# When the projections of a transposed block are queued in a four-layer graph network, and four edits of its first group

## The chip, the cores and the metric

The kernel runs on one core of a Trainium2 chip. Its time is device microseconds of one execution of the whole program; the reported number is the median of three runs. The profile is of one further execution.

## The reference

Four graph layers are applied to node features `x` (3327 x 256, float32) with one dense 0/1 adjacency `adj` (3327 x 3327). Each is wrapped as `x = layernorm(x + layer(x, adj))`. Cut to what matters:

```python
# layer 0: cosine attention, half of it kept
Qn, Kn = norm(x @ Wq.T), norm(x @ Wk.T)
att = softmax(where(adj > 0, Kn @ Qn.T, NEG), axis=1)
out0 = 0.5 * (att @ x) + 0.5 * x            # rows without neighbours keep x
# layer 1 and each of the three passes of layer 3 (3a, 3b, 3c): additive attention
h  = x @ W
e  = leaky_relu(h @ a[:D] + (h @ a[D:]).T, 0.01)
out = elu(softmax(where(adj > 0, e, NEG), axis=1) @ h)
# layer 2: dot-product attention
q, k, v = x @ Wq.T + bq, x @ Wk.T + bk, x @ Wv.T + bv
out2 = elu(softmax(where(adj > 0, q @ k.T / 16, NEG), axis=1) @ v)
```

Layer 3 first multiplies by `W0`, then makes the three passes, each on the result of the one before; only the end of the third is added to `x` and normalised.

## The kernel before, in words

**Tiles and loops.** The nodes are padded to 3328 = 26 tiles of 128 (`NT`). Rows are worked on in `NB` = 7 blocks: b = 0 to 5 have 512 rows (four tiles), b = 6 has 256 (two tiles). The program is one list of steps (layer, b, j): for each of six layer passes (keys "0", "1", "2", "3a", "3b", "3c"), each block b and each key tile j = 0 to 25. A step adds `e.T @ V[j]` to the accumulators `po` of the block, one matmul for each row tile (L1331; L1316 in the very last block of 3c; seven half-size products in L779 for layer 2 and the middle blocks of layer 0). A float32 matmul appears as two rows in the record. There are five `po` banks and three other banks (`bank()`, tag `pb`) of the accumulator memory.

**Weights ahead of their use.** The attention weights `e` of a step are made two steps earlier: ScalarE makes `re` (L657), VectorE multiplies it by the adjacency mask (L668). Before that a pass needs `th`, `rh`, `nrh` for its keys and `u` for the block's rows. They come from the end of the pass before: `shift` (a maximum on VectorE L606, a maximum over partitions on GpSimd L608, five small VectorE operations), `keys` (L623 to L627) and `block` (L649).

**Finishing a block.** `finish` is a generator that works on block b while the next block's steps run. `advance()` is called once at the end of each step and moves it to its next `yield`. For layers 1 and 3 it scales the accumulators into `p4` (L957, which frees the `po` banks), and then `turn` transposes `p4` by DMA. That is: ScalarE copies the two 16-bit halves into `planes` (L834), SP's queue issues the transposing DMA (L837), the generator yields `steps` times, and VectorE copies the arrived planes into `pT` (L844). After that each row tile is projected by TensorE with the layer's weights (`projected`, L988) and activated. So the number `steps` decides after which step's matmuls the first projection stands in the program. It is 3 for b = 0 to 4; for b = 5 and b = 6 it is 5 in layer 1 and 6 in layer 3. Block 5 is finished during block 6, whose steps hold half the matmuls; block 6 is finished during the first block of the next pass. At the end of block 5 come `shift`, `keys` and `rows` for the next pass.

In layer 1 the normalised block is turned a second time (L1063), for the keys of layer 2; that call has its own step numbers.

At step j = 20 (25 in the last block of layer 1) whatever is still pending is drained at once.

**Who sets the order.** Up to the fourth step the order of TensorE, ScalarE, VectorE and GpSimd is written by hand (`manual_schedule`). After that a planner orders each engine's instructions: it keeps its own model of how long things take, and of the instructions that this model says are ready it takes the one that comes first in the program. Each engine then runs its list in order, with semaphores. DMAs are issued from SP's queue, the first one also from ScalarE's.

**The start.** Six matmuls of ones (`turned`, "fills", L80) run first, then four that make the identity. `queries0(0)` multiplies the features into `pk` (two banks), takes lengths on ScalarE (L368) and an inverse root on VectorE (`rk`), scales the four tiles (`kr`: tile 0 on ScalarE L390, tiles 1 to 3 on VectorE L388), and transposes them on TensorE (`pkT`, L394). `keys0(0)` makes `pq` (L317), squares it on ScalarE (`qsq`, L324), copies it (L325), sums the squares with eight small matmul rows into `pn` (L329), and VectorE makes the inverse root `rq`, after the first adjacency mask (`take_adj`). The order of the two generators is a list in the main program:

```python
    for part in (k0, q0, k0, q0, q0, k0, k0, q0, q1):
        next(part, None)
```

## Time and profile before

| | |
|---|---|
| median of three runs | 2369.26 us (2368.96 to 2370.93) |
| profiled execution, its time | 2369.43 us |
| its span, first to last instruction | 2367.6 us |
| granted TensorE clock, mean | 0.998 |
| TensorE matmul, busy | 2343.5 us (99%) |
| TensorE weight loads, busy | 1914.2 us (81%) |
| VectorE, busy | 1598.5 us (68%) |
| ScalarE, busy | 1222.4 us (52%) |
| GpSimd, busy | 39.9 us (2%) |
| DMA, mean rate | 91 GB/s |

PE stands for TensorE, PEld for its weight loads, ACT for ScalarE, DVE for VectorE, POOL for GpSimd, SP for the engine whose queue issues DMAs. A row of a timeline reads: start in us, length in us, engine, line, operation, what is written from what is read, shape, number of instructions, and in brackets the idle time before it with what ended it. A row of waits reads: who waited for whom, us in total, times, longest. Matmuls are pipelined and the record models their ends, so TensorE's 99% says that it is always occupied and not that it is at its peak.

### The profile page before, as it was taken

The numbers are of one execution on the slowest core, as the hardware profiler recorded it, in microseconds if no ns is written. First come the engines' busy times: TensorE is split into PE (matmuls) and PEld (weight loads), VectorE is DVE, ScalarE is ACT, GpSimd is POOL, SyncE is SP. The second block draws the span as 40 slices with busy tenths as digits, with TensorE's granted clock in tenths as the row PEclk, the third lists the DMA queues.
The fourth block names the chain that finished last, engine by engine and source line by source line (L and its number), as shares of the span: only waits on it lengthen the run. The fifth ranks groups of instructions, "written<-read, shape, count | busy, mean of one in ns | idle before, by whom it ended". The sixth has DMA issues, their size and how long they took to land.

```text
span 2367.6 us, 33122 instructions
## 1 busy us (share of the span) xinstructions
PE 2343.5 (99%) x11961; PEld 1914.2 (81%) x11961; DVE 1598.5 (68%) x4246; ACT 1222.4 (52%) x1958; POOL 39.9 (2%) x156
## 2 busy tenths in 40 slices
PE   9999999999999999999999999999999999999997
PEld 6788888888888777667667798888888888888886
DVE  7789999856666667566566685556556555655655
ACT  4677777755555422222222255555655555655554
POOL 0000001000000000000000000000000000000000
PEclk9999999999999999999999999999999999999999
DMA  8655555413332312212212222211211111122120
GB/s 274 192 191 186 168 191 194 158 62 83 83 78 57 107 50 87 83 50 88 77 46 73 84 83 52 72 52 26 79 44 43 45 57 52 49 93 69 61 66 23
DMA packets 147288, 214.66 MB, mean 91 GB/s; under 512 B 76093, under 2 KB 101172, under 8 KB 142516
## 3 DMA queue, kind: packets, MB, share of 16 engines
q1 hardware_dynamic: 146852, 212.28, 29.2%
q8 instruction: 94, 1.54, 0.3%
q14 instruction: 70, 0.57, 0.1%
q10 hardware_dynamic: 272, 0.26, 0.0%
HBM read 167.53 MB, written 28.19 MB: 83 GB/s over the span
## 4 chain that ended last, share of the span: by engine, by line
PE 96%; DVE 2%; DMA 1%; ACT 1%; issue 0%; SPq 0%; POOL 0%; DVEq 0%; ACTq 0%
PE po L1331 50%; PE po L779 20%; PE ps L563 12%; PE ps L492 6%; PE pproj L988 4%; PE pv L1074 1%; PE pgq L522 1%; PE po L1316 1%; PE pk L353 1%; DMA stage<-in_adj_a 0%; PE pq L317 0%; DVE v L668 0%; DVE e L506 0%; DVE acc L449 0%; PE pn L329 0%
## 5 line engine op out<-in xcount | busy, mean ns | idle before, releaser
L1331 PE MATMUL po<-v,e 128*128 128x257 f32 x5616 | 1251.8, 381 | 1.5 <-ACT p L957 1.4
L1331 PEld LDWEIGHTS po<-v,e 128*128 128x128 f32 x5616 | 1062.1, 190 | 168.6 <-ACT p L957 9.4
L657 ACT ACTIVATE re<-u,nrh,th 128x512 f32<-128x512 f32 (+1 forms) x728 | 555.0, 780 | 479.2 <-DVE e L668 474.7
L668 DVE SCALAR_TENSOR_TENSOR e<-re,rh,mask 128x512 f32<-128x512 f32 (+1 forms) x702 | 501.1, 719 | 375.8 <-PE po L1331 353.1
L563 PE MATMUL ps<-gT,ft 128*128 128x512 f32 (+1 forms) x728 | 307.4, 563 | 0.0
L571 ACT ACTIVATE ex<-ps,off 128x512 f32<-128x512 f32 (+1 forms) x182 | 119.1, 656 | 357.2 <-PE ps L563 356.5
L779 PE MATMUL po<-tsums,ssum 128*128 128x128 f32 (+1 forms) x1794 | 249.3, 275 | 0.0
L477 DVE SCALAR_TENSOR_TENSOR e<-ex,mask 128x512 f32<-128x512 f32 (+1 forms) x182 | 118.5, 651 | 162.4 <-ACT ex L571 161.4
L779 PEld LDWEIGHTS po<-tsums,ssum 128*128 128x128 f32 x1794 | 224.5, 192 | 0.7 <-ACT y L913 0.3
L563 PEld LDWEIGHTS ps<-gT,ft 128*128 128x128 f32 x728 | 132.1, 190 | 114.5 <-issue 111.7
L779 PEld LDWEIGHTS po<-v,e 128*128 128x128 f32 x1196 | 169.3, 191 | 67.4 <-issue 54.2
L779 PE MATMUL po<-v,e 128*128 128x129 f32 x1196 | 182.4, 275 | 0.0
L505 ACT ACTIVATE ex<-ps,rq 128x512 f32<-128x512 f32 (+1 forms) x183 | 118.9, 652 | 115.8 <-PE ps L492 107.3
L492 PE MATMUL ps<-ft,ft 128*128 128x512 f32 (+1 forms) x312 | 142.4, 561 | 0.0
L506 DVE SCALAR_TENSOR_TENSOR e<-ex,mask 128x512 f32<-128x512 f32 (+1 forms) x183 | 116.7, 643 | 32.3 <-ACT ex L505 31.3
L449 DVE CUSTOM_DVE_ANT_0 acc<-acc,stage 128x1024 uint16<-128x1024 uint16 (+1 forms) x168 | 108.7, 647 | 13.1 <-DMA stage<-in_adj_a 10.0
L779 PE MATMUL po<-tsums,e 128*128 128x128 f32 x598 | 92.2, 275 | 0.4 <-DVE y L821 0.4
L779 PE MATMUL po<-v,ssum 128*128 128x128 f32 x598 | 92.3, 275 | 0.0
L436 ACT ACTIVATE mask<-pos 128x1024 uint8<-128x1024 bf16 (+1 forms) x87 | 86.3, 992 | 2.1
L435 ACT ACTIVATE pos<-stage 128x1024 bf16<-128x1024 int32 (+1 forms) x87 | 85.6, 983 | 1.2 <-DVE e L506 1.2
L988 PE MATMUL pproj<-w_l_w,pT 128*128 128x256 f32 x304 | 78.4, 381 | 4.6 <-DVE pT L844 4.6
L779 PEld LDWEIGHTS po<-tsums,e 128*128 128x128 f32 x598 | 79.3, 192 | 0.6 <-issue 0.6
(254 smaller groups left out, 1802.4 us busy)
## 6 DMA issues: line engine op xcount, KB each, us to landing
mask<-mask_d SPq DMA_DIRECT2D x30, 1664.0 KB
stage<-in_adj_a SPq DMA_DIRECT2D x78, 512.0 KB
tsums<-t_d SPq DMA_DIRECT2D x152, 256.5 KB
mask_d<-mask SPq DMA_DIRECT2D x6, 1664.0 KB
u<-s_d SPq DMA_DIRECT2D x24, 256.0 KB
xT<-in_xT SPq DMA_DIRECT2D x10, 512.0 KB
mask<-mask_d SPq DMA_DIRECT2D x5, 832.0 KB
t_d<-tsums SPq DMA_DIRECT2D x14, 256.5 KB
```

The source lines that it names most:

```text
L449: nc.vector.tensor_tensor(acc, acc, st[:, h * wd : (h + 1) * wd], ALU.add)
L477: nc.vector.scalar_tensor_tensor(e[:, :wd], t_[:, :wd], 0.0, mask(b, j), ALU.add, ALU.mult)
L492: nc.tensor.matmul(ps[:, :wd], FT[j // 4][:, 0, (j % 4) * P : (j % 4 + 1) * P], FT[b][:, 1, :wd], start=True, stop=True,)
L505: nc.scalar.activation(t_[:, c], ps[:, c], AF.Exp, scale=rq[:, j : j + 1])
L506: nc.vector.scalar_tensor_tensor(e[:, c], t_[:, c], 0.0, mask(b, j)[:, c], ALU.add, ALU.mult)
L563: nc.tensor.matmul(ps[:, :wd], FT[j // 4][:, h, (j % 4) * P : (j % 4 + 1) * P], g[:, h, :wd], start=(h == 0), stop=(h == 1),)
L571: nc.scalar.activation(t_[:, :wd], ps[:, :wd], AF.Exp, bias=off, scale=1.0 / D**0.5)
L657: nc.scalar.activation(t_[:, :wd], self.u[b][:, :wd], AF.Relu, bias=self.nrh[:, j : j + 1], scale=self.th[:, j : j + 1],)
L668: nc.vector.scalar_tensor_tensor(e[:, :wd], t_[:, :wd], self.rh[:, j : j + 1], mask(b, j), ALU.add, ALU.mult,)
L779: nc.tensor.matmul(o, x, y, start=(p == 0 and g not in banks[:i]), stop=(p == NT // 2 - 1 and g not in banks[i + 1 :]),)
L988: nc.tensor.matmul(pm[:, :D], pT[:, h, :], w[L.w][:, h, :], start=(h == 0), stop=(h == 1),)
L1331: nc.tensor.matmul(pos[k], es[:, k * P : (k + 1) * P], V[L.i % 2][j], start=(j == 0), stop=(j == NT - 1),)
```

## The change

Four edits. The step numbers of the turned rows move into a function: in layer 3 from 3 to 4 for b = 0 to 4, from 6 to 7 for b = 5, and from 6 to 4 for b = 6; in layer 1 they stay 3 for b = 0 to 4 and 5 for b = 5, and go from 5 to 3 for b = 6. The drain goes from j = 20 to j = 22 (it stays 25 in the last block of layer 1). At the start there are eight fills instead of six; the sums of the first group's keys, `pn0`, go to a bank of the `po` pool, so far unused at that point, and the first mask is taken after the inverse root instead of before; the scaling of the four tiles is shared two and two by ScalarE and VectorE instead of one and three.

```diff
     turned = bank("turned")
-    for _ in range(6):
+    for _ in range(8):
         nc.tensor.matmul(turned[:, :P], ones, ones, start=True, stop=True)
...
-        pn = bank("pn0")
+        pn = bank("pn0") if g > 0 else ps_o.tile([P, D + 1], F32, tag="po", name="pn0")
...
         if g == 0:
-            take_adj(0, 0)
             nc.vector.tensor_scalar(v[:, :n], pn[:, :n], COS_EPS * COS_EPS, None, ALU.max)
             rsqrt(rq[:, 4 * g : 4 * g + n], v[:, :n], n)
+            take_adj(0, 0)
...
-            if g == 0 and k > 0:
+            if g == 0 and k > 1:
                 nc.vector.tensor_scalar(kr[:, k, :], src[k], rk[:, k : k + 1], None, ALU.mult)
             else:
                 nc.scalar.mul(kr[:, k, :], src[k], rk[:, k : k + 1])
...
+    def turn_steps(L, b):
+
+        if L.key == "1":
+            return 5 if b == NB - 2 else 3
+        return 7 if b == NB - 2 else 4
...
-                    3 if b < NB - 2 else 5 if L.key == "1" else 6,
+                    turn_steps(L, b),
...
-        if j == (25 if L.key == "1" and b == NB - 1 else 20) and not end:
+        if j == (25 if L.key == "1" and b == NB - 1 else 22) and not end:
             while pending:
                 advance()
```

## The prediction

> **What bounds the kernel now.** I read the page first, then the waits of TensorE, then its timeline around each of those waits.

> ```profile
> PE 2343.5 (99%) x11961; PEld 1914.2 (81%) x11961; DVE 1598.5 (68%) x4246; ACT 1222.4 (52%) x1958; POOL 39.9 (2%) x156
> PE 96%; DVE 2%; DMA 1%; ACT 1%; issue 0%; SPq 0%; POOL 0%; DVEq 0%; ACTq 0%
> ```

> ```profile
> PE pproj L988 <- DVE pT L844: 5.3, 6, 1.4
> PE po L1331 <- ACT p L957: 1.4, 3, 0.5
> PE pn L329 <- ACT ft L325: 1.2, 1, 1.2
> PE turned L80 <- DVE ones L76: 1.1, 1, 1.1
> ```

> The first two lines (engine shares, chain) say that TensorE is the kernel: only 2367.6 - 2343.5 = 24.1 us of the span are not its work, and about 13.2 of those lie after its last matmul (2354.5). The change touches no matmul of the main loop, so it can only win from the remaining 10.9 us. The next four lines are TensorE's waits: 5.3 us in six waits of the projection L988 for the turned rows pT, 1.2 us at the start for pn. Those two entries are what the change aims at.

> The timelines of TensorE give the six. One (0.71 us, at 787.79) is in layer 1, whose numbers for that place stay. Five are in layer 3:

> ```profile
> 1692.57 1.13 PE L988 MATMUL pproj<-w,pT 128*128 128x256 f32 x4 [0.65 <-DVE pT L844]
> 1693.54 0.60 PE L1331 MATMUL po<-v,e 128*128 128x257 f32 x2
> ...
> 2088.94 1.13 PE L988 MATMUL pproj<-w_l_w,pT 128*128 128x256 f32 x4 [0.96 <-DVE pT L844]
> ...
> 2323.34 8.83 PE L1316 MATMUL po<-v,v 128*128 128x257 f32 x40
> 2333.57 1.13 PE L988 MATMUL pproj<-w_l_w,pT 128*128 128x256 f32 x4 [1.40 <-DVE pT L844]
> ```

> The other two are 0.59 us at 2011.94 and 0.95 us at 2285.12. So two kinds: 0.96 + 0.95 = 1.91 us in full blocks of layer 3c (finish of b = 0 and b = 4), and 0.65 + 0.59 + 1.40 = 2.64 us in the last blocks (finish of b = 5 in 3a, 3b, 3c).

> **Where a projection stands in TensorE's queue.** A matmul is two rows of the record (5616 rows of L1331 are 2808 matmuls), a row is 0.217 us. A step of a full block is 8 rows, 1.73 us; of the last block 4 rows, 0.87 us. I counted L1331 rows from each block's first to its first projection. In all full blocks of layer 3 it is 48 rows, 6.0 steps, exactly where the program puts it with steps=3. In the last blocks it is 42 rows, 10.5 steps (40 rows, 10.0, in 3c), although the program puts it at 9 with steps=6. The second to fourth projection stand at 11, 13, 15 as written. In layer 1, with steps=5 (place 8 in the program), the first is also at 10.5. I infer that there the planner, not the step number, sets the place: it takes the first projection only when its own model has pT ready.

> [...] during all five waits nothing behind L988 runs. [...] The trace has 94 packets of 1.54 MB on q8, 16 KB each[...]: windows 2079:2090 and 2275:2286 (the two late full blocks) hold one q8 packet beside the transpose, window 2129:2138 (on time) none. Copies start 4.3 us after the issue without it (2131.50 to 2135.78) and 6.0 us with it (2081.53 to 2087.53, 2277.73 to 2283.71). [...] In the timeline the 128-wide rows follow each other every 0.213 us until about 6.8 and every 0.111 us after. [...] VectorE's first scaling L388 waits 0.48 us for ScalarE's L390, though each reads other columns of pk.

> **The change, part by part.**

> *Full blocks of layer 3, 3 to 4 steps.* The projection moves from 6.0 to 7.0, 8 rows = 1.73 us later. At 2088.94 pT was ready 0.96 us late, at 2285.12 0.95 us: both are covered, 0.77 us to spare. Gain **1.91 us**. The ordinary blocks have no wait (copies end 1497.30, projection 1497.87), so nothing to win. [...] the reserve is then 0.57 + 1.73 = 2.3 us against a delay of 1.7, so it doesn't matter which block is met. The copies themselves, which block VectorE for 0.5 us until the transpose lands, keep their place; VectorE is 68% busy and its weights are up to five buffers ahead. DMAs: the transpose is issued where it was; the four output DMAs on SP's queue go one step later, nothing waits for them.

> *b = 5 of 3a, 3b, 3c, 6 to 7 steps.* Program place 9 becomes 10. That is still not above 10.5 and 10.0, so by the inference above the first projection stays, and so do the 2.64 us. Projections two to four go to 12, 14, 16: no wait there before, none after. Gain **0**; bounds 0 to 0.65 + 0.59 + 0.87 = 2.11 us if it does move one step. What follows is one step (0.87 us) later: in 3a and 3b the keys' shift. In the timeline mx is at 1703.44, u done at 1706.12, the next layer's first weights at 1707.76; TensorE asks for them at 1711.1. The one GpSimd item in it, am (0.51 us), moves with it, and GpSimd has nothing else there. Reserve 3.3 us, after it 2.5. Cost 0, at most 0.9 per boundary. In 3c the last rows of b = 5 leave at 2349.7 instead of 2348.8, before the tail's own output at 2359.43. The drain at j = 22 is what gives the longer finish room; at 20 it would have pulled the last item of the longer one forward.

> *b = 6, 6 to 4 (layer 1: 5 to 3).* These finish in the next layer's first block. Copies end at 1718.30 and 2037.88, projections stand at 1726.08 and 2045.45; two steps (3.5 us) earlier is 1722.6 and 2042.0, still behind. Layer 1: copies end 830.76, projection 841.93, two steps of 3.3 us earlier is 835.4. Gain and cost 0. The drain moves the mean row of layer 1 (pmean at 890.1) and the combination behind it, done at 894.83, some 6.6 us later; its product is asked for in the block's last pair, about 907. Reserve 5 us, so 0. In blocks 1 to 5 of layer 1 one pair of VectorE additions moves one step: 0.

> *The start* is written out by hand, so in order. Two fills are 4 rows at 0.213 = +0.85 us; 4 rows of pk then fall behind the clock's rise and take 0.111 instead of 0.213: -0.41. So pk, pq and qsq come **+0.44** us later (qsq ends 10.94 instead of 10.50; the columns for pk had landed by 5.6, so no idle time hides the fills). Before, pn waited for the copy L325 (ends 10.97) to free its bank and began at 11.02; in the unused bank it waits for qsq alone: 10.99. **-0.44** against the shift, and pn stands where it stood. (That bank is the fifth of the po buffers; block 0 holds the other four, and pn is read by 12.8.) Scaling two and two: rk at 11.23; ScalarE's pair ends 11.96, VectorE's, without the 0.48 us wait, 11.87; before the last ended at 12.14. The transposes pkT start behind pn at 11.94 as before. rq comes at 13.9 instead of 14.39, but the first exponential waits for ps (14.43). The mask behind rq may put the first weights from 15.4 to 15.7; TensorE reaches them at 16.84. Sum **0**; bounds -0.4 (if the clock or the data came later) and +0.5.

> Sum against the profiled execution: 2367.6 - 1.9 = 2365.7 span, 2369.43 - 1.9 = 2367.5 us. The runs shown have a median of 2369.26, 0.2 below, so **2367.3 us**.

> **Rivals.**

> *A, as above:* full blocks only, 2367.3. Chance 0.62.

> *B, the last blocks move too:* the planner's arrival shifts with the step. For it: 3c stands exactly at 10.0, on the edge. Against it: steps 5 and 6 gave the same 10.5. 2367.3 - 2.1 = 2365.2. Chance 0.15.

> *C, the gain doesn't show:* the change moves projections, but the two late blocks were this execution's, or the planner puts them elsewhere, or the fills cost their 0.44 and more. 2369.3. [...] Chance 0.13.

> *D, slower:* the layer ends of 3a and 3b. If the keys' chain, one step later, makes the planner put one more weight (L657, 0.80 us) ahead of the scaling p L957, which frees the bank that po waits for (0.54 us at 1711.67, 0.55 at 2031.05), each boundary costs 0.87 + 0.80 = 1.7 us, two 3.3; with the start's +0.5 and A's gain, 2369.3 - 1.9 + 3.8 = 2371.2. It decides from a delay above the 2.5 us reserve or from one ScalarE row in a changed order. A planner that reorders more widely would go beyond it. Chance 0.10.

> **The numbers.** The forecast is A. The range takes in B and its start's -0.4 (2364.8) and C with half of D (2370.4). About 0.2% (4.7 us) is what a measurement of this kernel can tell from no change. All five waits and the start's lower bound together would be 1.91 + 2.11 + 0.4 = 4.4 us, just inside, so faster by more is 0.05; slower by more needs D doubled, 0.07; within 0.88.

> **What would show it.** After: L988 waits for L844 four times instead of six, about 3.3 us (0.71, 0.65, 0.59, 1.40); first projections at 7.0 in full blocks and at 10.5, 10.5 and 10.0 in the last ones; pn without an ft L325 wait but starting near 11.0; two waits of po for L957 near 0.54. It is wrong if the last blocks' waits shrink (B), if L988 still waits in full blocks (C), or if the L957 waits or a wait of po for e grow (D).

## The result, and the profile after

The changed kernel takes **2367.19 us** (median of 22 runs, 2365.04 to 2368.11) against 2370.73 us for the kernel before on the same chip (22 runs, 2368.80 to 2371.97). The ratio is 0.9985 with a 95% interval of 0.9979 to 0.9992, that is 3.5 us less (1.9 to 5.0). The profiled execution took 2367.45 us with a span of 2365.6 us, where 2367.6 us was the span before.

Engine shares and chain of the page after:

```profile
PE 2342.0 (99%) x11965; PEld 1913.4 (81%) x11965; DVE 1598.1 (68%) x4245; ACT 1223.0 (52%) x1959; POOL 38.7 (2%) x156
PE 94%; DVE 3%; ACT 1%; DMA 1%; issue 1%; POOL 0%; SPq 0%; DVEq 0%; ACTq 0%
```

The waits of TensorE after (who waited for whom, us in total, times, longest; L994 was L988, L1337 was L1331, L963 was L957):

```profile
PE pasum L464 <- DVE af L460: 3.3, 3, 1.5
PE pproj L994 <- DVE pT L844: 3.3, 4, 1.4
PE po L1337 <- ACT p L963: 1.3, 2, 0.6
PE turned L80 <- DVE ones L76: 1.1, 1, 1.1
PE pn L329 <- ACT qsq L324: 0.7, 1, 0.7
```

The projections wait four times and 3.3 us instead of six times and 5.3 us. Also `pn` no longer waits for L325. But there is a line on top that the prediction does not have: `pasum`, the transposes of the adjacency sum in layer 0, waits 3.3 us. Before, it was

```profile
PE pasum L464 <- DVE af L460: 0.9, 1, 0.9
```

TensorE's timeline after, at one of the two full blocks of 3c and at the ends of 3a and 3c:

```profile
2084.76 5.36 PE L1337 MATMUL po<-v,e 128*128 128x257 f32 x24
2089.96 1.03 PE L994 MATMUL pproj<-w_l_w,pT 128*128 128x256 f32 x4
...
1692.81 1.13 PE L994 MATMUL pproj<-w,pT 128*128 128x256 f32 x4 [0.64 <-DVE pT L844]
...
2331.56 1.13 PE L994 MATMUL pproj<-w_l_w,pT 128*128 128x256 f32 x4 [1.42 <-DVE pT L844]
```

The projection at 2089.96 carries no bracket: nothing was idle ahead of it. Counted from each block's first L1337 row, first projections stand at 7.0 steps in full blocks, and at 10.5, 10.5 and 10.0 in the last blocks of 3a, 3b and 3c.

The start after, on TensorE (`po` is the first output product):

```profile
9.62 1.05 PE L329 MATMUL pn<-ones,qsq 128*128 128x1 f32 x8 [0.69 <-ACT qsq L324]
10.54 0.64 PE L394 MATMUL pkT<-ident,ft 128*128 128x128 f32 x4
15.44 1.90 PE L1337 MATMUL po<-v,e 128*128 128x257 f32 x8
```

and before:

```profile
11.02 1.05 PE L329 MATMUL pn<-ones,qsq 128*128 128x1 f32 x8 [1.16 <-ACT ft L325]
11.27 0.87 DVE L388 TENSOR_SCALAR ft<-pk,rk 128x128 f32<-128x128 f32 x3 [0.48 <-ACT ft L390]
11.94 0.64 PE L394 MATMUL pkT<-ident,ft 128*128 128x128 f32 x4
16.84 0.38 PE L1331 MATMUL po<-v,e 128*128 128x257 f32 x1
```

The first output product comes 1.40 us earlier, and `pn` does too; from `pn` on both take 5.82 us. In this execution the clock rose to full at 4.10 us, before at 6.87; up to the rise TensorE's 128-wide rows follow each other every 0.213 us, behind it every 0.111 us. In layer 0 the changed kernel's profile then loses more than the 1.40 us: at 93.98 and 168.24 TensorE waits 1.29 and 1.50 us for a sum that VectorE finished late, after it had waited for an adjacency tile.

```profile
91.48 1.42 DVE L449 CUSTOM_DVE_ANT_0 acc<-acc,stage 128x1024 uint16<-128x1024 uint16 x2 [2.89 <-DMA stage<-in_adj_a]
93.41 0.42 DVE L460 CAST af<-acc 128x512 f32<-128x512 int32 x1
93.98 0.63 PE L464 MATMUL pasum<-ident,af 128*128 128x128 f32 x4 [1.29 <-DVE af L460]
```

VectorE sat idle for 2.89 us until the last tiles had come (2.47 us at the same place before), adds them, converts the sum, and TensorE stands behind both.

So these two profiles alone do not show where the gain comes from. The projections wait 2.0 us less and the sums 2.4 us more. The 2.0 us between the spans are mostly busy time of TensorE, 1.5 us less (2343.5 to 2342.0), which may be the earlier rise of the clock; two profiles do not show that it is.

### The profile page after: what moved, and what is told of

Same layout as the page of the kernel before. It is cut to its first block, busy times and chain, and to the rows that moved or that the text cites. A ratio compares the mean times of both kernels' runs of the same rounds, so it can differ in the third digit from the quotient of the medians.

```text
span 2365.6 us, 33125 instructions
## 1 busy us (share of the span) xinstructions
PE 2342.0 (99%) x11965; PEld 1913.4 (81%) x11965; DVE 1598.1 (68%) x4245; ACT 1223.0 (52%) x1959; POOL 38.7 (2%) x156
## 3 DMA queue, kind: packets, MB, share of 16 engines
q8 instruction: 94, 1.54, 0.3%
## 4 chain that ended last, share of the span: by engine, by line
PE 94%; DVE 3%; ACT 1%; DMA 1%; issue 1%; POOL 0%; SPq 0%; DVEq 0%; ACTq 0%
PE po L1337 49%; PE po L779 19%; PE ps L563 12%; PE ps L492 6%; PE pproj L994 3%; PE pv L1080 1%; PE pgq L522 1%; ACT re L657 1%; PE po L1322 1%; PE pk L353 0%; PE pq L317 0%; DVE e L668 0%; DMA stage<-in_adj_a 0%; DVE v L668 0%; DVE e L506 0%
## 5 line engine op out<-in xcount | busy, mean ns | idle before, releaser
L1337 PE MATMUL po<-v,e 128*128 128x257 f32 x5616 | 1251.7, 381 | 1.4 <-ACT p L963 1.3
L1337 PEld LDWEIGHTS po<-v,e 128*128 128x128 f32 x5616 | 1062.2, 190 | 168.4 <-issue 9.3
L657 ACT ACTIVATE re<-u,nrh,th 128x512 f32<-128x512 f32 (+1 forms) x728 | 555.4, 780 | 472.2 <-DVE e L668 466.9
L449 DVE CUSTOM_DVE_ANT_0 acc<-acc,stage 128x1024 uint16<-128x1024 uint16 (+1 forms) x168 | 108.5, 646 | 15.4 <-DMA stage<-in_adj_a 11.8
L994 PE MATMUL pproj<-w_l_w,pT 128*128 128x256 f32 x304 | 78.2, 380 | 2.7 <-DVE pT L844 2.7
L779 PEld LDWEIGHTS po<-v,ssum 128*128 128x128 f32 x598 | 79.4, 192 | 0.1
```

Of the source, the lines that this page charges most:

```text
L449: nc.vector.tensor_tensor(acc, acc, st[:, h * wd : (h + 1) * wd], ALU.add)
L657: nc.scalar.activation(t_[:, :wd], self.u[b][:, :wd], AF.Relu, bias=self.nrh[:, j : j + 1], scale=self.th[:, j : j + 1],)
L779: nc.tensor.matmul(o, x, y, start=(p == 0 and g not in banks[:i]), stop=(p == NT // 2 - 1 and g not in banks[i + 1 :]),)
L994: nc.tensor.matmul(pm[:, :D], pT[:, h, :], w[L.w][:, h, :], start=(h == 0), stop=(h == 1),)
L1337: nc.tensor.matmul(pos[k], es[:, k * P : (k + 1) * P], V[L.i % 2][j], start=(j == 0), stop=(j == NT - 1),)
```

## The experiments

Twelve kernels were run, each in five rounds beside the kernel before. Medians are compared through the ratio to the kernel before on the same chip.

### The full blocks alone, and the ends alone

```diff
-                    3 if b < NB - 2 else 5 if L.key == "1" else 6,
+                    (3 if L.key == "1" else 4) if b < NB - 2 else 5 if L.key == "1" else 6,
```

> The kernel before, with the turned rows of layer 3 at 4 steps in blocks 0 to 4 and nothing else changed. My theory (full blocks carry layer 3's gain): no wait of L988 for L844 in full blocks, first projections at 7.0 steps there and at 10.5, 10.5, 10.0 in the last blocks with waits near 0.65, 0.6 and 1.4; 1.9 us faster than before. Rival (the start carries most of what was measured): the same places, but under 1 us faster. Rival (all four edits are needed together): no measurable gain.

Measured: 2367.87 us, ratio 0.9992 (0.9984 to 1.0001), span 2366.6. Its waits of TensorE:

```profile
PE pproj L988 <- DVE pT L844: 3.4, 4, 1.4
PE pasum L464 <- DVE af L460: 3.2, 2, 2.0
```

Both full-block waits are gone and the four others stay (5.3 less 3.4 is 1.9 us). By the ratio the kernel is 1.9 us faster (the medians as they stand differ by 2.6). The interval alone does not exclude zero, nor the rival of under 1 us. The span of the profile is only 1.0 us shorter, since `pasum` waits 2.3 us more than before, though nothing at the start was changed here.

```diff
-                    3 if b < NB - 2 else 5 if L.key == "1" else 6,
+                    3 if b < NB - 2 else 5 if L.key == "1" else 7 if b == NB - 2 else 6,
...
-        if j == (25 if L.key == "1" and b == NB - 1 else 20) and not end:
+        if j == (25 if L.key == "1" and b == NB - 1 else 22) and not end:
```

> The kernel before, with the turned rows of layer 3's block 5 at 7 steps and the drain at j = 22, nothing else. My theory (the planner's own arrival sets the first projection's place): still 10.5, 10.5 and 10.0 steps, waits near 0.65, 0.6 and 1.4, time the same within 0.4 us. Rival (one step more moves it): first projections at 11.0 or later, waits 0.4 to 0.9 us shorter each, about 2 us faster.

Measured: 2370.48 us, ratio 1.0002 (0.9993 to 1.0010). The waits of the ends are 0.64, 0.57 and 1.42 us, those of the full blocks are back at 0.98 and 0.94. So a step more at the ends moves nothing that this measurement shows. The clock held a surprise, in the windows of this profile (stretch, its length, busy time of PE, PEld, DVE, ACT, POOL, then the granted clock; the stretches are 3.41 us each, counted from its rise):

```profile
4.76:8.17 3.41, 3.41 (x24) 2.79 (x24) 0.42 (x2) 1.47 (x8) 0.00 (x0) 1.00 1.04 386
8.17:11.59 3.42, 2.26 (x15) 1.57 (x14) 2.70 (x14) 1.34 (x3) 0.00 (x0) 1.00 1.06 404
11.59:15.00 3.41, 3.41 (x5) 1.31 (x5) 2.24 (x12) 0.71 (x2) 0.00 (x0) 0.50 1.05 375
```

The clock rose early, at 4.76, and **fell back** to half at 11.59 for 3.41 us, after a stretch in which TensorE was busy for 2.26 us. From `pn` to the first output product it took 7.37 us (10.02 to 17.39), where the profiles before and after, without a fall there, have 5.82 us: in this profile the fall goes with 1.55 us more.

### The four start edits

All four on the kernel before, the step numbers left as they were. The edits are those of the change.

> The kernel before, with the four edits of the start (eight fills, the sums in a free bank, the mask behind the inverse root, scaling two and two) and nothing of layer 3 or the drain. My theory: the fills cost 0.44 and the bank gives 0.44, time the same within 0.5 us; the clock's rise lies at a place that differs from run to run, and sets where pn stands. Rival (eight fills make the clock rise earlier, 4.1 us as in the profile of the changed kernel instead of 6.9): clock at 4.1 again, pn near 9.6, about 1.4 us faster than before.

Measured: 2367.75 us, ratio 0.9988 (0.9980 to 0.9997), 2.8 us less (0.7 to 4.7). Not zero, so "the same within 0.5 us" is a miss. The clock rose at 4.12, as the rival says, but with the same eight fills it rose at 6.76 and 7.16 in other runs below, so the fills do not set the rise. In the profile the two full-block waits are also shorter, 0.55 and 0.14 us, although their step number is as before. If 1.2 us of the gain is put down to them, about 1.6 is left for the start; that is an estimate from one profile, in which `pasum` waits 2.3 us more. The gains of the full blocks alone and of the start alone, 1.9 and 2.8, are 1.2 us more than the 3.5 of the whole change: what the start edits take off the full-block waits is not there a second time, as far as intervals this wide can say.

The changed kernel with six fills again:

```diff
-    for _ in range(8):
+    for _ in range(6):
```

> The changed kernel with six fills instead of eight, all else as changed. My theory (a fill costs its rows whatever the clock does): 0.44 us faster than the changed kernel, so 3.9 us faster than before; projections at 7.0, 10.5, 10.5, 10.0. Rival (eight fills bring the clock's rise forward): clock at 6.9 as before and 1 us or more slower than the changed kernel, so 2 to 2.5 us faster than before.

Measured: 2366.42 us, ratio 0.9985 (0.9978 to 0.9991). The two fills make no difference to the median that this measurement shows; neither the 0.44 us expected nor the rival's loss can be seen. But the mean clock is 0.997 in 6 of these 21 runs, and three of the six took 2369.7 to 2370.2 us; the changed kernel has no such run in 22. Then the bank alone and the fills alone, on the kernel before:

```diff
-        pn = bank("pn0")
+        pn = bank("pn0") if g > 0 else ps_o.tile([P, D + 1], F32, tag="po", name="pn0")
```

> The kernel before, with the sums of the first keys in the free bank, nothing else (six fills, scaling one and three, mask ahead of the root). My theory now (TensorE's idle stretch before pn, 1.16 us, lets the clock fall back to half for 3.4 us when its rise came early; 0.69 us does not): the stretch is 0.69 us, no fall-back, 1 to 1.5 us faster than before at the median. Rival (the bank is worth its 0.44 us alone): 0.4 us faster.

Measured: 2370.21 us, ratio 0.9999 (0.9991 to 1.0007). The gain expected did not come. TensorE's and VectorE's timeline shows where it went:

```profile
10.58 1.05 PE L329 MATMUL pn<-ones,qsq 128*128 128x1 f32 x8 [0.69 <-ACT qsq L324]
...
11.30 0.87 DVE L388 TENSOR_SCALAR ft<-pk,rk 128x128 f32<-128x128 f32 x3 [0.48 <-ACT ft L390]
11.49 1.06 PE L394 MATMUL pkT<-ident,ft 128*128 128x128 f32 x4
...
16.82 0.38 PE L1331 MATMUL po<-v,e 128*128 128x257 f32 x1
```

`pn` begins 0.44 us earlier, but the four transposes now take 1.06 instead of 0.64 us: they wait for VectorE's three scalings, which still stand behind ScalarE's. The wait was moved, not removed. The theory's "no fall-back" is not borne out either: the mean clock is 0.998 in 5 of the 13 runs and 0.996 in 4, a mean that among the profiles only the one with two falls has.

```diff
-    for _ in range(6):
+    for _ in range(8):
```

> The kernel before, with eight fills, nothing else. My theory (a fill costs its rows and does nothing for the clock): stretch before pn still 1.16 us, clock's rise anywhere between 4.1 and 6.9, 0.4 us slower than before at the median. Rival (the fills keep the clock up): no fall-back and 1 us or more faster than before.

Measured: 2371.05 us, ratio 1.0003 (0.9995 to 1.0011). The rival's gain of 1 us or more is not seen. In this profile too the clock falls back:

```profile
10.17:13.58 3.41, 2.25 (x15) 1.58 (x14) 2.71 (x13) 1.91 (x4) 0.00 (x0) 1.00 1.03 391
13.58:17.00 3.42, 3.42 (x5) 1.51 (x5) 2.31 (x10) 0.85 (x3) 0.00 (x0) 0.50 0.69 241
```

The bank with the scaling, and the scaling alone:

```diff
-            if g == 0 and k > 0:
+            if g == 0 and k > 1:
```

> The kernel before with the keys' sums in the output pool and the scaling split two and two; six fills and the old place of the mask. Theory now: the bank alone shifts the sums 0.44 us earlier (idle before them 0.69 instead of 1.16 us), but the first transposes then wait for VectorE's three scalings; with both edits the first scores and the first output product come 0.44 us earlier after the sums, and no stretch of 3.41 us holds less than about 2.6 us of TensorE work, so that the clock does not fall back to half in any run. That gives 0.44 us in each run and 1.5 us in those runs of the kernel before in which the clock falls back: 1 to 2.5 us at the median, ratio 0.9989 to 0.9996, profile with a single rise of the clock, pn to first po L1331 5.8 us. Rival: the gain of the four start edits came from the two more fills and the later mask; then ratio 0.9997 to 1.0003, and a fall of the clock may be seen.

Measured: 2368.88 us, ratio 0.9993 (0.9985 to 1.0001). A single rise of the clock, at 4.62, and 5.82 us from `pn` to `po` (9.47 to 15.29). The profile agrees with the theory, the median too (1.6 us less), but the interval does not exclude zero and so does not shut the rival out.

> The kernel before with only the scaling split two and two; the keys' sums stay in the bank that is evicted first. Theory: the idle time before the sums stays 1.16 us, and after the sums VectorE was not late (no wait ahead of the fifth transpose), so nothing moves: ratio 0.9998 to 1.0003[...]. Rival: the split scaling alone shortens the stretch between the sums and the first scores by the 0.44 us: ratio 0.9993 to 0.9998.

Measured: 2374.37 us, ratio 1.0016 (1.0010 to 1.0023): both expectations fall, the edit **costs** 3.9 us. Its timeline in layer 0, and the windows around its second fall of the clock:

```profile
93.48 0.39 SPq L931 DMA_DIRECT2D mask_d<-mask  x1
95.00 0.33 SPq L424 DMA_DIRECT2D stage<-in_adj_a  x1
96.71 1.42 DVE L449 CUSTOM_DVE_ANT_0 acc<-acc,stage 128x1024 uint16<-128x1024 uint16 x2 [3.06 <-DMA stage<-in_adj_a]
...
99.21 0.63 PE L464 MATMUL pasum<-ident,af 128*128 128x128 f32 x4 [3.30 <-DVE af L460]
```

```profile
7.95:11.36 3.41, 2.25 (x15) 1.45 (x14) 3.03 (x16) 1.60 (x4) 0.00 (x0) 1.00 1.06 401
...
96.70:100.11 3.41, 0.90 (x6) 0.69 (x7) 2.56 (x5) 0.00 (x0) 0.00 (x0) 1.00 1.02 352
100.11:103.52 3.41, 3.41 (x8) 2.01 (x7) 1.91 (x5) 0.69 (x1) 0.00 (x0) 0.50 0.56 232
```

The order of TensorE's work is the same as before, but SP's queue issues several adjacency loads (L424) at other places, and VectorE's order differs too. TensorE waits 3.30 us for the adjacency sum, and the clock falls twice, at 11.36 and at 100.11. These are most of what this profile loses; that the moved loads are the reason is not shown. With the bank added (the run above) SP's order differs from before in nearly the same places, without that loss.

The last of this group tests the fall-back itself. Work without a purpose fills TensorE's idle time ahead of `pn` in the kernel before:

```diff
+        if g == 0:
+            fill = ps_o.tile([P, D + 1], F32, tag="po", name="fill")
+            for _ in range(4):
+                nc.tensor.matmul(fill[:, :P], ones, ones, start=True, stop=True)
         pn = bank("pn0")
```

> The kernel before with four matmuls of ones more on TensorE between the last matmul into pq and the sums pn, into the fifth po bank, which nothing else uses there; pn keeps its bank and still waits for the copy L325, the scaling is as before. They take 4 x 0.22 = 0.9 of the 1.16 us that TensorE is idle there, so nothing behind them moves. Theory (the clock falls back when a stretch of 3.41 us holds too little TensorE work: 2.25 or 2.26 us where it fell, 2.60 or more where it didn't): that stretch now holds some 3.1 us, so there is no fall-back in the profile whenever the clock rises; the mean granted clock is 0.998 in most runs, where it is 0.997 or 0.996 in three runs of four of the kernel before, and the median is 0.5 to 1.5 us lower, ratio 0.9994 to 0.9998. Rival (the fall-back comes from something else, or the stretch from pn to the first scores sets it): clock means spread as those of the kernel before, ratio 0.9998 to 1.0004.

Measured: 2366.79 us, ratio 0.9984 (0.9978 to 0.9991), 3.75 us less. The mean granted clock is 0.998 in 19 of 21 runs, in the kernel before beside it in 5 of 25. The stretch is full now:

```profile
9.67:13.08 3.41, 3.14 (x23) 2.25 (x21) 2.72 (x14) 1.86 (x4) 0.00 (x0) 1.00 0.99 384
```

So filling the stretch goes with a clock that stays up in most runs. The profile itself is a weak test: its clock rose at 6.26, between the rises of the start before after which the clock fell (4.76) and after which it did not (6.72 and 6.87). The gain is larger than expected, and not all of it is the clock: in this profile nearly half of it is the full blocks' waits, 0.24 us and nothing instead of 0.96 and 0.95, 1.7 us shorter. How the rest divides is open. The runs at 0.998 are 3.2 us below the kernel before's at 0.998 (2366.79 against 2370.02), but some of these may have an early rise, and the one early rise recorded with the start before (4.76) was followed by a fall, so that comparison does not part the clock from the rest.

### What was left on the table

The ends of layer 3 two steps later, drain and next layer's first projections with them, on the changed kernel:

```diff
-        return 7 if b == NB - 2 else 4
+        return 9 if b == NB - 2 else 4
...
-        begin = 2 if last and b == NB - 2 else 14
+        begin = 2 if last and b == NB - 2 else 16 if L.key in ("3a", "3b") and b == NB - 1 else 14
-        if j == (25 if L.key == "1" and b == NB - 1 else 22) and not end:
+        if j == (25 if L.key == "1" and b == NB - 1 else 24 if L.key in ("3a", "3b") and b == NB - 1 else 22) and not end:
```

> The changed kernel with block 5 of layer 3 at 9 steps instead of 7 (in 3a and 3b the next pass's rows then load from j = 16 and the drain is at j = 24 in block 6). My theory: the program's place, 12, is now behind the planner's arrival, so the first projections stand at 12.0; their waits (0.64, 0.59, 1.42) vanish, 2.6 us faster than the changed kernel, 6.1 us faster than before. Rival (the keys' chain, two steps of 0.87 us later, runs out of its reserve): the wait of po for the scaling of p, or one for e, grows by 0.8 us or more at each of two layer ends, and under 1 us is left of the gain.

Measured: 2364.39 us, ratio 0.9972 (0.9963 to 0.9982), 2.8 us below the changed kernel. Its waits of TensorE:

```profile
PE po L1337 <- DVE e L668: 2.0, 2, 1.0
PE pasum L464 <- DVE af L460: 1.6, 1, 1.6
...
PE pproj L994 <- DVE pT L844: 0.7, 1, 0.7
```

Once the place really moves, the three waits of the ends (2.65 us) go. The next late thing is then the first weights of the next pass: 1.0 us at each of two boundaries, in place of 0.64 us for `p`.

The adjacency sum two steps later in layer 0, on the changed kernel:

```diff
-        if L.key == "0" and j == NT - 1 - LA:
+        if L.key == "0" and j == NT - 1:
```

> The changed kernel with the adjacency sums of layer 0 (af, pasum) made at the end of step j = 25 instead of j = 23, nothing else. My theory (TensorE waits there only because pasum stands in front of matmuls that are ready): the waits of pasum for af (3.3 us in three in the changed kernel's profile) fall under 1 us, 2 to 3 us faster than the changed kernel. Rival (the adjacency's DMA is late anyway, so the next user waits): waits of po or ps for e or ex appear in layer 0 of about the same sum, no gain.

Measured: 2364.46 us, ratio 0.9975 (0.9965 to 0.9984), 2.7 us below the changed kernel; no wait of `pasum` is left in the profile. The rival's waits in its place do not come. So the 3.3 us of `pasum` after were on the path. All together, with six fills:

> The changed kernel with six fills, the ends of layer 3 two steps later (turned rows 9 steps ahead of use at b = 5, in 3a and 3b the next layer's first projections begin at step 16 and the drain at 24), and the last layer-0 sum of the adjacency at step NT-1. Theory: the gains are at different places of the span and add up: 2.8 us for the ends (2364.39 against 2367.19), 2.7 us for the sum (2364.46), 0.0 to 0.8 for the fills (2366.42): 2361 to 2362, ratio 0.9962 to 0.9970. Rival: the later sum and the later ends shift when the adjacency and mask transfers meet the turning ones, and part is given back elsewhere: 2363 to 2364.5.

Measured: **2361.49 us** (5 runs), ratio 0.9960 (0.9947 to 0.9974), 9.5 us less than the kernel before (6.2 to 12.6). The gains add up within what five runs can tell. Its waits of TensorE:

```profile
PE po L1337 <- DVE e L668: 2.0, 2, 1.0
PE turned L80 <- DVE ones L76: 1.1, 1, 1.1
PE pn L329 <- ACT qsq L324: 0.7, 1, 0.7
PE pproj L994 <- DVE pT L844: 0.7, 1, 0.7
```

## Why the prediction was right, and where it was not

**Full blocks: right in the mechanism, and in size for the profile before.** 1.91 us was the sum; alone it measured 1.9 us (between 0.2 slower and 3.8 faster), with the places at 7.0 and no wait. But 1.91 us is no constant of the program: at three steps the two waits together are 1.03 us with the bank alone and 0.97 with bank and scaling, kernels with not one matmul more, and 0.5 to 0.7 with eight fills, which the changed kernel has.

**b = 5: right, and for its reason.** Places 10.5, 10.5 and 10.0, waits 0.64, 0.59 and 1.42. That the planner and not the step number holds the place is borne out from both sides: 7 steps change nothing, 9 steps do.

**b = 6 and the drain: right.** First projections at 7.0 and 8.0 steps of the next block, no wait. The scaling `p` at the boundaries waits 0.64 instead of 0.54 us.

**The start: the term that failed.** Its sum was 0 (bounds -0.4 and +0.5). The terms were right for the clock rise that the one profile showed. With a rise at 7.16 and all four edits (the kernel with late ends) `pn` began at 11.09 and `po` at 16.90; before, with the rise at 6.87, 16.84: a difference of 0.06. With six fills and a rise at 6.88 (all together) `po` came at 16.38, so bank and scaling bring 0.46 and the fills take about as much. The failed step is the one that took the rise from a single execution and let nothing follow from it: "the 128-wide rows follow each other every 0.213 us until about 6.8". The twelve profiles of the experiments and the two others have it anywhere from 4.10 to 7.16. In the profile of the start before with an early rise the clock fell back to half (rise at 4.76: `po` at 17.39), and so it did with the scaling shared (rise at 4.53: 17.28) and with eight fills (rise at 6.76: 18.83). With the start after and an early rise it did not (4.10 and 4.12: 15.44 and 15.45; with six fills, 4.72). Up to the first output product that is 1.95 us between the early rises of 4.76 and 4.10, and the 0.06 us above between the late ones. The prediction's bounds allowed only for a later rise. At the median the start is worth 0.7 us (changed kernel against full blocks alone, medians as they stand) to 1.6 us (by their ratios, and from the experiment with the bank and the scaling).

**Not seen at all:** the adjacency sums. VectorE waits there for tiles (2.47 us before, 2.89 after, 3.06 with the scaling alone), and what TensorE waits for `pasum` differs from one profile to the next: 0.9 us before, 3.3 after. It would be natural to say that an earlier TensorE meets a tile that the DMA has not delivered. The runs do not show that: the full blocks alone, with `po` at 16.77, wait 3.2 us, the fills alone, with `po` at 18.83, 2.7 us, and bank and scaling, with `po` at 15.29, 1.9 us. What sets the size stays open; that it costs time is shown by the later sums.

**The rivals.** B falls by the places (the last blocks do not move at 7 steps), C by the full blocks alone, where the waits go, though the median's interval leaves it some room; its doubt that the two waits were this execution's was half right, since their size changes. D falls here (two waits for `p` of 0.64 us, no new one), but the lateness it feared is real: at 9 steps `po` waits for the next pass's weights, 1.0 us at each boundary. The forecast of 2367.3 us lies 0.1 us above the changed median, but the kernel before ran at 2370.7 beside it and not at 2369.26: the change is 1.6 us larger than the 1.9 forecast, about what the start brings. That the time came out so close is luck: the median of three runs was 1.5 us low, and the start's gain was missing.

**Why the turned rows of 3c arrive late.** That the q8 packets would stand beside the same two blocks again was an assumption of the prediction. In the profile after they do: a packet begins beside the transposes of b = 0 and b = 4 and beside none of the other four, as before. Before, it begins 3.98 and 3.97 us after the issue, and VectorE's copy 6.00 and 5.98 us after it; in the profile after, the packet begins after 2.65 and 2.17 us and the copy after 5.53 and 5.20. The eight transposes without a packet, in both profiles together, have the copy 4.28 to 4.37 us after the issue. The profiles of the start alone, the bank alone, the fills alone and the filled stretch have one q8 packet each in the windows of the same two transposes. So the wait changes under edits elsewhere, and none of the six profiles with four steps has a full-block wait. No run moved the packet by itself: that it delays the transpose is not shown.

## What to carry to other kernels

Before counting on a moved step, ask who decides the place: if a planner's own arrival time holds the instruction, a larger step number does nothing until it passes that time. A wait at the start can go with more than its length: in the run of the ends alone, 1.16 us of waiting for `pn` were followed by a fall of the clock and 1.55 us more up to the first output product. One profile of the start shows one time of the clock's rise, and here it lay anywhere from 4.10 to 7.16 us: look at several. A wait behind a chain of two (here a bank and a scaling) may go only when both are mended. And a wait read in one profile need not be the wait of the next run: the full-block waits and the adjacency sums changed by 0.9 to 2.3 us under edits that do not touch them.

## What the runs showed of the hardware

```profile
92.87:96.28 3.41, 1.45 (x7) 1.00 (x8) 2.53 (x6) 0.00 (x0) 0.00 (x0) 1.00 0.86 304
```

while at the start it fell after 2.25 or 2.26 us. In the run of the ends alone, the window of the start for line L329 by itself (PE, PEld, clock, DMA) is

```profile
8.17:11.59 3.42, 1.05 (x8) 0.97 (x8) 1.00 1.06 404
```

so that 1.05 us of the 2.26 us are the sums `pn`, whose rows have a single column each (128x1). Whether the kind of work makes the difference is not shown, since no run varied it by itself; the filled stretch above has more work altogether (3.14 us), and no fall behind it. What decides when the clock falls stays open.

Beside the twelve experiments the kernel before ran 141 times: mean clock 0.998 in 34 (median 2369.90 us), 0.997 in 97 (2370.58), 0.996 in 10 (2372.68). The changed kernel ran at 0.998 in all 22. The mean does not part falls from anything else that lowers it, so these counts are no count of falls alone; but the slowest group is 2.8 us above the first. Up to the first output product, the same start edits go with 0.06 us between the profiles with rises at 6.87 and 7.16 and with 1.95 us between those at 4.76 and 4.10.
